# Two graph layers: row sums written over adj's transpose, a norm placed later, a copy moved to ScalarE

## The chip, the cores and the metric

One core of a Trainium2 chip runs the kernel. The metric is the device time in microseconds, the median of several executions. Beside it stands one profiled execution, from which all durations are taken.

TensorE is PE in the profile (PEld is its weight load), VectorE DVE, ScalarE ACT, GpSimd POOL, SyncE SP. L12 means line 12 of the kernel before.

## The reference

64 graphs of 256 nodes with 256 features go through two layers, each with a residual and a layer norm. Cut to what matters:

```python
# layer 0
deg = adjacency_matrix.sum(axis=-1)
deg = jnp.where(deg != 0, deg, 1.0)
d_inv_sqrt = deg ** (-0.5)
norm_adj = d_inv_sqrt[:, :, None] * adjacency_matrix * d_inv_sqrt[:, None, :]
a_plus = norm_adj + alpha_eff * jnp.eye(N)
h = jnp.einsum('bnm,bmf->bnf', a_plus, x)
x = _layernorm(x + jnp.einsum('bnf,pf->bnp', h, W) + b)
# layer 1
h = relu(bn1(conv1d(xc, conv1_w, 0)))            # xc: x with channels ahead of nodes
h = bn2(conv1d(h, conv2_w, 8))                   # 17 taps over the nodes
x_conv = relu(h + xc)
s = x @ w_se.T + b_se                            # 3 columns
dist = sq[:, :, None] + sq[:, None, :] - 2.0 * jnp.einsum('bnd,bmd->bnm', s, s)
A = jnp.exp(-dist) * adj
x_nmp = jnp.einsum('bnm,bmd->bnd', A, relu(x @ w_msg.T + b_msg))
x = _layernorm(x + gru(concat([x_conv, x_nmp]), x))
```

## The kernel before

Everything is float32. The 64 graphs run in four groups of 16 (Q = 16). A graph's work is written as Python generators, whose `yield`s are the places where other work is put in between.

- `layer0(g)` loads are two graphs deep (`loads`, two buffers for adj_t and x_t). Row sums of adj (`degrees`, L357: two ACT instructions with `accum_out`, whose written output isn't used), deg and adeg on DVE (L368, L372), deg to the power -0.5 on POOL (L370). TensorE transposes adj (L379), ACT copies it to adjT (L380; blocks 0 and 2 of each row of three), DVE puts the diagonal in the middle block (L382), ACT scales x (L392). Then p_hT (L400), hT (ACT, L405), p_out (L410), the residual on DVE (L415). `layernorm` takes statistics on DVE (L326 to L328), the root on POOL (L329), a product on DVE (L332), and applies them on ACT (L334); x1 goes to memory (L421).
- `layer1(g)` transposes x1 (L430) to xn (L434 on DVE, L435 on ACT), then p_conv (L450) with two readers on ACT (h L453, scols L454), p_msg (L471, msg L474 on ACT), a Fourier transform of tiles of h (p_dft, L486, copied out by ACT in L491), p_rows (L499: transposes of the three columns and their squares). Rows 0 to 63 of p_rows go to dist_l by ACT (L501), rows 64 to 127 to dist_r: by ACT (L504) for the 12 graphs in `ALONE` (16 to 27), by DVE (L506) for the other 52. p_dist (L513) multiplies them, ACT takes the exponential (L514), DVE multiplies with adjT (aT, L515), p_nmp (L522) and its copy (L526) end the layer.
- The 17-tap convolution is a product in the frequency domain (`products`, p_k L548) once for each group, with transforms on DVE (L598 to L735). `gru(g)` follows (p_g, L874, with sums on POOL, L845).
- In the first group, `weights` computes the transform of the convolution's weights as "other" work between the pieces: taps scaled on DVE (L300), p_u (L308), copied to u_set by ACT (L311), a difference on DVE (L313), a sum on POOL (L314), written out by POOL's queue (L316).

adjT has three buffers, x1 two, the banks for p_rows, p_dist and others four in common (`ps`).

`graphs` sets the order: while layer1 of graph i runs, layer0 of graph i + 2 is taken forward one piece at the places that `PLACES` names. Its last part, the applied norm, is kept in `ENDS` and run during the next graph's layer1, before that one's piece number `APPLIED` is followed by others. The order in which instructions stand on each engine is then settled by a scheduler when the kernel is built: it takes whatever is ready by its own reckoning, in order of its place in the program, so that an instruction may stand earlier or later than the text has it. L357 of a graph stands one or two graphs ahead of its transposes in this way, since its output `unused` is always free.

Of the kernel before, what the change touches and what calls it, by code (L numbers as in the profile page):

```python
# [10 lines left out]
AF = mybir.ActivationFunctionType  # L11
# [3 lines left out]
P = 128  # L15
# [11 lines left out]
def kernel(  # L27
# [27 lines left out]
    nc = tc.nc  # L55
# [291 lines left out]
    def layer0(g):  # L347

        a_t, x_t = ain.pop(g), xin.pop(g)

        adjT = work.tile([P, NCH, 3, P], F32, name="adjT", bufs=3)
        ADJT[g] = adjT

        deg = small.tile([P, NCH], F32, name="deg")
        def degrees():
            for c in range(NCH):
                nc.scalar.activation(  # L357
                    unused, a_t[:, c, :], AF.Copy,
                    accum_out=deg[:, c : c + 1],
                )  # L360

        if g == 1:

            with tc.issue_after(X_SCALED[0]):
                degrees()
        else:
            degrees()
        nc.vector.scalar_tensor_tensor(deg, deg, 0.0, deg, op0=ALU.is_equal, op1=ALU.add)  # L368
        dis = small.tile([P, NCH], F32, name="dis")
        nc.gpsimd.tensor_tensor(dis, deg, neg_half[:, :NCH], op=ALU.pow)  # L370
        adeg = small.tile([P, NCH], F32, name="adeg")
        nc.vector.tensor_scalar(adeg, deg, alpha_t, None, op0=ALU.mult)  # L372

        p = bank("p_adjT").rearrange("p (c n) -> p c n", c=NCH)
        for mc in range(NCH):
            for c in range(NCH):
                nc.tensor.transpose(p[:, mc, c * P : (c + 1) * P], a_t[:, c, mc * P : (mc + 1) * P], ident)  # L379
        copied = nc.scalar.copy(adjT[:, :, 0:3:2, :], p.rearrange("p c (n q) -> p c n q", q=P))  # L380
        for mc in range(NCH):
            DIAGONAL[g] = nc.vector.scalar_tensor_tensor(  # L382
                adjT[:, mc, 1, :], ident, adeg[:, mc : mc + 1], adjT[:, mc, 2 * mc, :],
                op0=ALU.mult, op1=ALU.add,
            ).ins


        x1 = work.tile([P, NCH, D], F32, name="x1")
        X1[g] = x1
        with tc.issue_after(copied.ins) if g < 2 else ExitStack():  # L390
            for c in range(NCH):
                X_SCALED[g] = nc.scalar.activation(x1[:, c, :], x_t[:, c, :], AF.Copy, scale=dis[:, c : c + 1]).ins  # L392
        nc.gpsimd.tensor_tensor(x_t, x_t, b0_t.unsqueeze(1).to_broadcast([P, NCH, D]), op=ALU.add)  # L393

        yield
        hT = work.tile([P, DCH, N], F32, name="hT", bufs=1)
        p = bank("p_hT").rearrange("p (k n) -> p k n", k=DCH)
        for k in range(DCH):
            for mc in range(NCH):
                nc.tensor.matmul(  # L400
                    p[:, k, :], x1[:, mc, k * P : (k + 1) * P],
                    adjT[:, mc, 1 - mc : 3 - mc, :].rearrange("p n q -> p (n q)"),
                    start=mc == 0, stop=mc == NCH - 1,
                )
        nc.scalar.copy(hT, p)  # L405
        yield
        p = bank("p_out0").rearrange("p (c o) -> p c o", c=NCH)
        for c in range(NCH):
            for k in range(DCH):
                nc.tensor.matmul(  # L410
                    p[:, c, :], hT[:, k, c * P : (c + 1) * P], w0[:, k, :], start=k == 0, stop=k == DCH - 1
                )
        for c in range(NCH):
            mark(
                nc.vector.scalar_tensor_tensor(  # L415
                    x1[:, c, :], p[:, c, :], dis[:, c : c + 1], x_t[:, c, :], op0=ALU.mult, op1=ALU.add
                )
            )
        yield
        yield from layernorm(x1)  # L420
        nc.scalar.dma_start(x1_d[g // Q][g % Q].rearrange("(c p) d -> p c d", p=P), x1)  # L421
        yield
# [14 lines left out]
    def layer1(g, place):  # L437

        if g not in XN:
            x1_transposed(g)  # L440
        xn, adjT = XN.pop(g), ADJT.pop(g)
        x1T = xn[:, 0 : 2 * DCH : 2 * DCH - 1]
        yield

        h = work.tile([P, NCH, D], F32, name="h", bufs=1)
        cols = scols.rearrange("p c (q r) -> p c q r", r=32)
        for c in range(NCH):
            p = bank("p_conv1")[:, : D + NSE]
            for k in range(DCH):
                nc.tensor.matmul(  # L450
                    p, x1T[:, k, c * P : (c + 1) * P], wc1[:, k, :], start=k == 0, stop=k == DCH - 1
                )
            nc.scalar.activation(h[:, c, :], p[:, :D], AF.Relu)  # L453
            nc.scalar.copy(cols[:, c, :, :NSE], p[:, D:].unsqueeze(1).to_broadcast([P, 4, NSE]))  # L454

        s3 = cols[:, :, 0, :NSE]
        sq3 = small.tile([P, NCH, NSE], F32, name="sq3")
        nc.vector.scalar_tensor_tensor(sq3, s3, -1.0, s3, op0=ALU.mult, op1=ALU.mult)
        nsq = small.tile([P, NCH], F32, name="nsq")
        nc.vector.tensor_reduce(nsq, sq3, AX.X, ALU.add)  # L460
        last = nc.vector.tensor_scalar(
            cols[:, :, 2:4, NSE], nsq.unsqueeze(2).to_broadcast([P, NCH, 2]), 0.5, None, op0=ALU.mult
        )
        mark(last)
        mark(last)
        yield
        msg = work.tile([P, NCH, D], F32, name="msg", bufs=1)
        p = bank("p_msg").rearrange("p (c d) -> p c d", c=NCH)
        for c in range(NCH):
            for k in range(DCH):  # L470
                nc.tensor.matmul(  # L471
                    p[:, c, :], x1T[:, k, c * P : (c + 1) * P], wmsg[:, k, :], start=k == 0, stop=k == DCH - 1
                )
        mark(nc.scalar.activation(msg, p, AF.Relu))  # L474
        yield


        mid = GT // 2
        if TILES[0] is not V:
            AWAY.append(place)  # L480
        for k in range(DCH):
            p = bank("p_dft")

            for c, t0, t1 in ((0, 0, mid + 1), (1, mid - 1, GT)):
                first = t0 + 1 - c * mid
                nc.tensor.matmul(  # L486
                    p[:, t0 * FL : t1 * FL], h[:, c, k * P : (k + 1) * P],
                    fwd[:, first : first + t1 - t0, :].rearrange("p t f -> p (t f)"),
                    start=c == 0, stop=True, skip_group_check=c == 1,
                )  # L490
            nc.scalar.copy(  # L491
                TILES[0][:, :, k, place * GT : (place + 1) * GT],
                p[:, : GT * FL].rearrange("p (t f) -> p f t", f=FL),
            )

        yield
        p = bank("p_rows")
        for c in range(NCH):
            nc.tensor.transpose(p[:, c * P : (c + 1) * P], scols[:, c, :], ident)  # L499
        dl = work.tile([64, N], F32, name="dist_l", bufs=1)  # L500
        nc.scalar.copy(dl, p[0:64, :N])  # L501
        dr = work.tile([64, N], F32, name="dist_r", bufs=1)
        if g in ALONE:
            nc.scalar.copy(dr, p[64:P, :N])  # L504
        else:
            nc.vector.tensor_copy(dr, p[64:P, :N])  # L506
        yield

        aT = work.tile([P, NCH, 2, P], F32, name="aT", bufs=1)
        for c in range(NCH):  # L510
            rows = slice(32 * c, 32 * c + 32)
            p = bank("p_dist")[:, :N]
            nc.tensor.matmul(p, dl[rows, c * P : (c + 1) * P], dr[rows, :], start=True, stop=True)  # L513
            nc.scalar.activation(aT[:, c].rearrange("p n q -> p (n q)"), p, AF.Exp, bias=nsq[:, c : c + 1], scale=2.0)  # L514
        mark(nc.vector.tensor_mul(aT, aT, adjT[:, :, 0:3:2, :]))  # L515
        yield
        if g in ALONE:
            x1_transposed(g + 1, True)
        p = bank("p_nmp").rearrange("p (k n) -> p k n", k=DCH)
        for k in range(DCH):  # L520
            for mc in range(NCH):
                nc.tensor.matmul(  # L522
                    p[:, k, :], msg[:, mc, k * P : (k + 1) * P], aT[:, mc].rearrange("p n q -> p (n q)"),
                    start=mc == 0, stop=mc == NCH - 1,
                )
        nc.scalar.copy(xn[:, 1 : 1 + DCH], p)  # L526
        nc.scalar.dma_start(xn_d[g], xn)
        yield
# [460 lines left out]


    PLACES = (("other",), ("layer0",), (), (), ("layer0",), ("other", "layer0"), ())
    STATS, APPLIED = len(PLACES) - 1, 2
    ENDS = [iter(())]

    def graphs(first, part, others):
# [219 lines left out]
```

## Time and profile before

| | us |
|---|---|
| median of 3 executions | 2115.55 |
| lowest and highest | 2112.75, 2115.77 |
| the profiled execution | 2121.38 |
| its span, first to last instruction | 2119.6 |

The span by stage, from PE's work: the first group's graphs with the weights until about 300 us, its frequency products with graphs 16 to 27 in between until about 520, then graphs and GRU steps in turn, and from about 1660 us only GRU steps and the last group's products. The two costliest groups of instructions, with count, total and mean time, and the idle time of the engine ahead of them:

```profile
L874 PE MATMUL p_g<-wall,sums 128*128 128x384 f32 x1536 | 538.8, 491 | 7.2 <-DVE G L901 7.2
L874 PE MATMUL p_g<-wall,inputs 128*128 128x384 f32 x1152 | 407.4, 490 | 14.3 <-DVE G L892 14.3
```

And what ACT waited for at the row sums, in total, how many times, and the longest:

```profile
ACT unused L357 <- DMA adj_t<-in_adj_dram: 41.0, 24, 5.2
```

The mean granted clock of TensorE was 0.986 of full speed.

### The profile page before, as it was taken

What the parts mean: (1) busy time and instruction counts of PE and PEld (TensorE: products, weight loads), DVE (VectorE), ACT (ScalarE), POOL (GpSimd) and SP (SyncE); (2) the same over time, 40 slices, a digit from 0 to 9 for tenths busy, and PEclk for the clock granted to TensorE, in tenths of its full rate; (3) what the DMA queues carried; (4) which work ended last, traced back from release to release, by engine and by line L of the source; (5) the groups of instructions that cost most, each with busy time, mean ns of one, the idle gap of its engine ahead of it and who ended that gap; (6) DMA issues with size and microseconds to landing.
All of it is one profiled execution on the core that took longest, in us unless ns stands there. A gap on an engine that the chain in (4) does not pass through costs nothing. (4 is left out here: it accounts for less than half of the span.)

```text
span 2119.6 us, 26193 instructions
## 1 busy us (share of the span) xinstructions
PE 2012.2 (95%) x8157; PEld 1448.3 (68%) x8157; DVE 1463.9 (69%) x3333; ACT 906.1 (43%) x2128; POOL 671.3 (32%) x672
## 2 busy tenths in 40 slices
PE   6999899999999999999999999999999999999997
PEld 5888678877667756767667765667767765555554
DVE  5555368676468788873546888885444889976776
ACT  4666543477431233555453123455444123333333
POOL 3445310121431243323221233332322124334453
PEclk9999899999999999999999999999999999999999
DMA  4765556545437644344325654434332855443331
GB/s 122 221 221 186 156 164 224 173 135 157 129 106 220 200 128 119 124 121 119 95 90 157 202 173 125 134 108 126 100 90 80 250 152 149 115 116 94 95 95 55
DMA packets 305289, 298.05 MB, mean 141 GB/s; under 512 B 84192, under 2 KB 283956, under 8 KB 305150
## 3 DMA queue, kind: packets, MB, share of 16 engines
q1 hardware_dynamic: 245198, 200.37, 32.3%
q10 hardware_dynamic: 44480, 67.39, 8.9%
q0 software_dynamic: 15472, 28.61, 6.1%
q8 instruction: 66, 1.08, 0.2%
q14 instruction: 73, 0.60, 0.1%
HBM read 193.19 MB, written 103.06 MB: 140 GB/s over the span
## 5 line engine op out<-in xcount | busy, mean ns | idle before, releaser
L874 PE MATMUL p_g<-wall,sums 128*128 128x384 f32 x1536 | 538.8, 491 | 7.2 <-DVE G L901 7.2
L874 PE MATMUL p_g<-wall,inputs 128*128 128x384 f32 x1152 | 407.4, 490 | 14.3 <-DVE G L892 14.3
L874 PEld LDWEIGHTS p_g<-wall,sums 128*128 128x128 f32 x1536 | 285.2, 191 | 197.5 <-issue 16.7
L874 PEld LDWEIGHTS p_g<-wall,inputs 128*128 128x128 f32 x1152 | 217.2, 191 | 166.8 <-DVE G L892 23.8
L845 POOL TENSOR_TENSOR sums<-inputs 128x384 f32<-128x384 f32 x128 | 139.5, 1090 | 342.4 <-PE p_g L874 314.0
L329 POOL TENSOR_TENSOR ln_rs<-ln_rs,neg_half 128x2 f32<-128x2 f32 x129 | 95.0, 737 | 391.4 <-DVE ln_rs L328 303.5
L916 ACT ACTIVATE G<-G 128x512 f32<-128x512 f32 x128 | 80.9, 632 | 263.1 <-DVE G L903 144.1
L548 PE MATMUL p_k<-u,VM 128*128 128x256 f32 x736 | 175.8, 381 | 2.4 <-DMA u<-ud 2.4
L548 PEld LDWEIGHTS p_k<-u,VM 128*128 128x128 f32 x736 | 139.4, 191 | 29.4 <-issue 2.7
L400 PE MATMUL p_hT<-adjT,x 128*128 128x256 f32 x512 | 129.9, 397 | 11.1 <-ACT msg L474 6.2
L370 POOL TENSOR_TENSOR dis<-deg,neg_half 128x2 f32<-128x2 f32 x64 | 47.3, 738 | 290.4 <-DVE deg L368 290.0
L450 PE MATMUL p_conv<-wc,xn 128*128 128x259 f32 x512 | 128.2, 391 | 11.5 <-DVE xn L434 10.6
L393 POOL TENSOR_TENSOR x_t<-x_t,b_t 128x512 f32<-128x512 f32 x64 | 94.4, 1476 | 135.8 <-issue 111.4
L410 PE MATMUL p_out<-w,hT 128*128 128x256 f32 x512 | 126.3, 390 | 1.8 <-ACT hT L405 1.3
L486 PE MATMUL p_dft<-fwd,h 128*128 128x240 f32 x512 | 117.0, 372 | 11.2 <-ACT scols L454 11.2
L522 PE MATMUL p_nmp<-aT,msg 128*128 128x256 f32 x512 | 122.6, 382 | 0.5 <-DVE aT L515 0.5
L450 PEld LDWEIGHTS p_conv<-wc,xn 128*128 128x128 f32 x512 | 96.3, 192 | 38.2 <-DVE xn L434 15.5
L471 PE MATMUL p_msg<-wmsg,xn 128*128 128x256 f32 x512 | 121.6, 380 | 0.0
L334 ACT ACTIVATE x_g<-x_g,ln_mr,ln_rs 128x256 f32<-128x256 f32 x128 | 71.0, 597 | 112.0 <-DVE ln_mr L332 110.2
L410 PEld LDWEIGHTS p_out<-w,hT 128*128 128x128 f32 x512 | 97.8, 194 | 29.4 <-ACT hT L405 9.5
L845 POOL TENSOR_TENSOR sums<-inputs,sums 128x384 f32<-128x384 f32 x64 | 69.1, 1079 | 146.6 <-PE p_g L874 146.3
L400 PEld LDWEIGHTS p_hT<-adjT,x 128*128 128x128 f32 x512 | 96.0, 198 | 27.9 <-ACT msg L474 10.9
(163 smaller groups left out, 3545.5 us busy)
## 6 DMA issues: line engine op xcount, KB each, us to landing
u<-ud SPq DMA_DIRECT2D x284, 256.0 KB
xn_d<-xn ACTq DMA_DIRECT2D x64, 512.0 KB
inputs<-xn_d SPq DMA_DIRECT2D x64, 512.0 KB
ud<-u_set POOLq DMA_DIRECT2D x39, 480.0 KB, 6.7
adj_t<-in_adj_dram SPq DMA_DIRECT2D x64, 256.0 KB
x_t<-in_x_dram SPq DMA_DIRECT2D x64, 256.0 KB
x_d<-x ACTq DMA_DIRECT2D x64, 256.0 KB
xc_d<-VM SPq DMA_DIRECT2D x64, 256.0 KB
```

What stands on the lines that cost most here:

```text
L329: nc.gpsimd.tensor_tensor(rs[:, : len(chunks)], rs[:, : len(chunks)], neg_half[:, : len(chunks)], op=ALU.pow)
L393: nc.gpsimd.tensor_tensor(x_t, x_t, b0_t.unsqueeze(1).to_broadcast([P, NCH, D]), op=ALU.add)
L400: nc.tensor.matmul(p[:, k, :], x1[:, mc, k * P : (k + 1) * P], adjT[:, mc, 1 - mc : 3 - mc, :].rearrange("p n q -> p (n q)"), start=mc == ...
L410: nc.tensor.matmul(p[:, c, :], hT[:, k, c * P : (c + 1) * P], w0[:, k, :], start=k == 0, stop=k == DCH - 1)
L450: nc.tensor.matmul(p, x1T[:, k, c * P : (c + 1) * P], wc1[:, k, :], start=k == 0, stop=k == DCH - 1)
L471: nc.tensor.matmul(p[:, c, :], x1T[:, k, c * P : (c + 1) * P], wmsg[:, k, :], start=k == 0, stop=k == DCH - 1)
L486: nc.tensor.matmul(p[:, t0 * FL : t1 * FL], h[:, c, k * P : (k + 1) * P], fwd[:, first : first + t1 - t0, :].rearrange("p t f -> p (t f)") ...
L522: nc.tensor.matmul(p[:, k, :], msg[:, mc, k * P : (k + 1) * P], aT[:, mc].rearrange("p n q -> p (n q)"), start=mc == 0, stop=mc == NCH - 1,)
L548: nc.tensor.matmul(p[:, j * D : (j + 1) * D], v[:, k, :], u[:, k, :], start=k == 0, stop=k == DCH - 1)
L845: nc.gpsimd.tensor_tensor(S[i], x, y, op=op)
L874: nc.tensor.matmul(p[:, : 3 * HD] if k == 0 else p[:, HD:], a[:, k], wall[:, b, k].rearrange("p t d -> p (t d)"), start=first and k == 0, ...
L916: nc.scalar.activation(rz, rz, AF.Tanh, scale=0.5)
```

## The change

Three edits. For the first 16 graphs the unused output of the row sums goes to the first two blocks of adjT of the same graph, which the copy L380 and the diagonal L382 later write over. The copy to dist_r is done by ACT for all graphs. The part of layer 0 behind its statistics (L332, L334, L421) is run at piece 4 of the next graph's layer1, after the copies of p_rows, instead of at piece 2, after p_msg.

```diff
         def degrees():
             for c in range(NCH):
                 nc.scalar.activation(
-                    unused, a_t[:, c, :], AF.Copy,
+                    unused if g >= Q else adjT[:, c, 0:2, :].rearrange("p n q -> p (n q)"), a_t[:, c, :], AF.Copy,
                     accum_out=deg[:, c : c + 1],
                 )
...
         dr = work.tile([64, N], F32, name="dist_r", bufs=1)
-        if g in ALONE:
-            nc.scalar.copy(dr, p[64:P, :N])
-        else:
-            nc.vector.tensor_copy(dr, p[64:P, :N])
+        nc.scalar.copy(dr, p[64:P, :N])
         yield
...
     PLACES = (("other",), ("layer0",), (), (), ("layer0",), ("other", "layer0"), ())
-    STATS, APPLIED = len(PLACES) - 1, 2
+    STATS, APPLIED = len(PLACES) - 1, 4
```

## The prediction

> **What bounds the kernel now.** I read the page's head first, then what TensorE waits for, then the dist_r tile, then the timeline of the two longest stalls.
>
> ```profile
> span 2119.6 us, 26193 instructions
> PE 2012.2 (95%) x8157; PEld 1448.3 (68%) x8157; DVE 1463.9 (69%) x3333; ACT 906.1 (43%) x2128; POOL 671.3 (32%) x672
> ```
>
> TensorE is busy for 95% of the span. A change pays only where TensorE stands still, or where its clock falls. All idle time of PE is about 107 us (2119.6 - 2012.2). The waits of TensorE (total, times, longest):
>
> ```profile
> PE p_g L874 <- DVE G L892: 14.3, 14, 3.0
> PE p_dist L513 <- DVE dist_r L506: 11.3, 10, 2.8
> PE p_dft L486 <- ACT scols L454: 11.2, 7, 2.3
> PE p_conv L450 <- DVE xn L434: 10.6, 9, 2.4
> ...
> PE p_hT L400 <- ACT msg L474: 6.2, 7, 4.5
> ```
>
> The change can touch the second line (dist_r), and whatever a late row sum (L357) delays. From the tile view of dist_r:
>
> ```profile
> L506 DVE COPY dist_r<-p_rows x52: 425/426/427, 41.6 to 1638.5; 64x256 f32<-64x256 f32 x52
> L504 ACT COPY dist_r<-p_rows x12: 369/370/371, 315.5 to 510.6; 64x256 f32<-64x256 f32 x12
> ...
>   ACT dist_l L501: 98.2, 40
> ```
>
> The last line says that DVE waited 98.2 us in front of dist_r for ACT's dist_l: the two copies read one bank and already run one after the other. The 11.3 us are thus no measure of the gain. Most of it is dist_l itself being late. The longest case, in the timeline:
>
> ```profile
> 237.66 0.42 ACT L357 ACTIVATE unused<-adj_t 128x256 f32<-128x256 f32 x1 [3.41 <-DMA adj_t<-in_adj_dram]
> 238.08 0.46 ACT L491 COPY VM<-p_dft 128x384 f32<-128x384 f32 x1
> 238.44 0.37 ACT L501 COPY dist_l<-p_rows 64x256 f32<-64x256 f32 x1
> 238.84 0.42 DVE L506 COPY dist_r<-p_rows 64x256 f32<-64x256 f32 x1 [5.34 <-ACT dist_l L501]
> 239.31 0.70 PE L513 MATMUL p_dist<-dist_r,dist_l 32*128 32x256 f32 x4 [2.83 <-DVE dist_r L506]
> ```
>
> ACT waits 3.41 us for the landing of an adj_t that is needed only two graphs later, and dist_l stands behind it. The windows view (us, then busy time per engine, clock, DMA) shows the sequel, a half clock:
>
> ```profile
> 235.35:240.70 5.35, 2.52 (x14) 1.62 (x13) 0.83 (x3) 2.67 (x9) 0.71 (x1) 1.00 0.29 96
> 240.70:244.10 3.40, 3.40 (x10) 2.63 (x9) 1.12 (x2) 1.36 (x3) 0.39 (x1) 0.50 0.03 6
> ```
>
> An ordinary graph of the first group, D = start of its p_dist = 125.78:
>
> ```profile
> 126.51 0.84 ACT L514 ACTIVATE aT<-p_dist,nsq 128x256 f32<-128x256 f32 x2
> 127.24 0.41 ACT L357 ACTIVATE unused<-adj_t 128x256 f32<-128x256 f32 x1
> 127.38 0.69 DVE L515 TENSOR_TENSOR aT<-aT,adjT 128x512 f32<-128x512 f32 x1 [1.11 <-ACT aT L514]
> ...
> 128.19 1.05 ACT L311 COPY u_set<-p_u 120x512 f32<-120x512 f32 x2
> ...
> 129.28 1.23 DVE L313 TENSOR_TENSOR u_set<-u_set,u_set 120x1024 f32<-120x1024 f32 x1 [0.50 <-ACT u_set L311]
> 129.32 3.40 POOL L314 TENSOR_TENSOR u_set<-u_set,u_set 120x1024 f32<-120x1024 f32 x1
> ```
>
> From L313 a DVE chain (L415, L326, L327, L328, L434) ends in xn at 133.19, 3.91 us after L313 starts. p_conv needs xn and could start at 133.64: 0.45 us of room.
>
> **What the Trainium skill says.** "TensorE: Matmul & The Clock Gate", on HAM oscillation, says that a TensorE gap over about 3.4 us lets the clock fall to half. The trace agrees in kind: 3.4 us at 0.50 after the stall at 239.31, and 10.2 us after the one at 258.69. It isn't strict: shorter stalls also did it (1.95 us at 420.02), and others of 2.45 us did not. "SBUF — State Buffer", in Who interferes with whom, says that a VectorE instruction with two SBUF inputs and a GpSimd instruction that reads SBUF lock each other out, the first holding the port. The trace agrees: L300 takes 1.21 us normally, and 3.37 us when it starts at 65.14 under POOL's L314 (64.04 to 67.43). "Perfetto Trace Analysis", Identifying the Most-Contended Engine, warns that matmul busy share isn't distance to the limit. So I price a stall as the time between two starts less the usual spacing (0.216 us for 256 columns: eight in 1.89 us, the last 0.38 long) and not busy time.
>
> **Part 1, row sums over adjT (g < 16).** The operations and their 0.42 us stay. Their output now needs a slot of adjT. There are three, and the oldest is freed by the aT product L515. In the built order of instructions the row sums of each graph therefore move back by about one graph: behind the exps and the first u_set copy, before the second. No queue of SP or POOL changes its sequence, save the small L370.
> Gains. At graph 12 the row sums of graph 15 and 16 stand behind the first u_set copies instead of ahead of dist_l: the stall at 239.31 (2.99 us against the usual spacing, 0.09 normal) goes, -2.9, and the 3.4 us at half clock after it, -1.7. The stall before p_conv at 228.74 (0.97, u_set copies behind a row sum that waited 1.46 for DMA) goes, -0.95. Two graphs in between with such waits of 0.6 us and 0.23 us longer spacing (15.88 against 15.65): -0.35 in all. At the start graph 1's second row sum comes before its adjT copy, so its x is ready earlier: -0.4 of 0.86.
> Costs. Row sums start at D+2.34 (after L515), the second u_set copy ends at D+3.88, and L313 starts at D+3.93 instead of D+3.50. The 0.45 us of room just covers that: nothing in graphs 2 to 11. At graph 0 the row sums used to stand before p_dist; now L313 slips 0.8 and p_conv at 49.87 waits 0.8 more. At graph 1 the taps product L300 moves ahead of L313, so L313 falls under POOL's L314 and ends about 1.2 later than the chain does now: +1.2, and the stall of 1.5 at 68.56 (p_u for taps) only moves to p_conv.
> The 4.69 us stall at 258.69 (ACT msg behind graph 17's row sum, which waits 5.23 for DMA) stays: graphs from 16 on keep their place, and the load is still issued about 9 us before.
> Sum: -2.9 -1.7 -0.95 -0.35 -0.4 +0.8 +1.2 = -4.3 us.
>
> **Part 2, dist_r by ACT (52 copies).** The wait between the two copies falls from 33 to 12 ns (the 12 copies of L504 show it) and the copy from 426 to 370 ns: 77 ns where dist_r ends the wait of p_dist and DVE was idle. Over nine such graphs 0.69, and 0.11 from two where the stall is smaller. Where DVE was busy with other work first, more goes: 0.91 at 612.25 (dist_r 0.87 us behind dist_l), 0.52 and 0.53 at 830.17 and 1343.01 (1.3 us behind, the whole stall), 0.28, 0.27, 0.12, 0.12 and 0.05 at 294.63, 1130.93, 875.21, 1388.05 and 1639.00. Sum -3.6. On ACT 52 x 0.37 = 19 us are added. They lie in the wait for p_hT (hT starts at its end in most graphs) or for L823's inputs; where hT has no room (0.05 us in graphs 41, 57 and 59) it could cost 0.37 each: taken at +0.5, bounds 0 and +1.1. At 957 and 1471 the built order puts L515 ahead of a late row sum on DVE: -0.6 for two stalls of p_nmp.
>
> **Part 3, norm at piece 4.** The scheduler moves only four norms (graph indexes near 418, 524, 792 and 1305 us). At 420.02 dist_l and dist_r come 0.6 earlier, but hT now stands behind norm and row sum and p_out comes 0.45 later: +0.45. At 526 exps come 0.4 earlier: -0.25. The other two move 33 us back, into 1.14 us of ACT idle time before 828.03: nothing, at most 0.5 each way. Sum +0.2.
>
> Total -4.3 -3.6 +0.5 -0.6 +0.2 = -7.8 us. Against the profiled execution, 2121.38 -> 2113.6. That execution lay 5.8 us above the median of 2115.55, so I carry the difference: 2107.7.
>
> **Rivals.** (a) Given back: half-clock stretches fall elsewhere once all phases shift. The trace has 47.8 us of them between 60 and 2100 us, 3.4 us each in nine places, each worth 1.7; two or three more, or the u_set room overdrawn by 0.4 us in ten graphs, leave 2113. For it: stalls of the same length are hit or not. Against: two long stalls fewer. (b) More: graph 17's load lands early enough once graph 15 and 16 are off ACT, and 4.7 us of stall with 5.1 of half clock go too: 2098. For it: other adj_t loads land within 3.2 us (307.04 to 310.2). Against: its place relative to POOL's writes of ud is unchanged. (c) Slower: POOL's L314 wins the port over L313. Today L313 starts 40 ns earlier. If the row sums, which now wait for L515, push adeg (L372, ahead of L313 on DVE) behind the start of L314, L313 waits out 3.4 us instead of taking 1.2, 2.2 more in each of ten graphs: +22 on the forecast, 2130. It decides from the point where L313 is later than D+4.3, when POOL's L370 ends; I have D+3.93. (d) The change not acting as it says: part 3 does little in the built order, already priced.
>
> **How the numbers follow.** Forecast 2107.7, own range 2102 to 2112, chance 0.64 (0.58 of it beyond 0.2%); (a) 0.14 (0.12 of it within); (b) 0.10; (c) 0.12. 0.2% is 4.2 us, about what repeated measurements can tell from no change. Faster 0.58+0.10+0.02 = 0.70, same 0.06+0.12 = 0.18, slower 0.12. The range 2096 to 2118 takes in (a) and (b) and leaves out (c).
>
> **What would show it.** Right: no wait of L513 near 236, ACT's L357 waiting for adj_t less than 41.0 us in all, p_dist's wait for dist_r at 5 us or less, L313 near D+3.9 in 1.23 us. Wrong: L313 at 3.4 us in many graphs, p_conv's wait for xn above 15 us, p_out waiting for hT by several us, or the 258.69 stall gone.

## The result and the profile after

| | before | after |
|---|---|---|
| median of 5 executions each, us | 2115.77 | 2103.45 |
| lowest and highest, us | 2112.75, 2117.18 | 2101.34, 2108.64 |
| profiled execution, us | 2121.38 | 2108.64 |
| its span, us | 2119.6 | 2106.8 |
| mean granted clock in it | 0.986 | 0.989 |

The ratio is 0.995 with a 95% interval of 0.993 to 0.997. The forecast was 2107.7, in a range of 2096 to 2118. Lines behind L503 stand three lower in the kernel after (dist_r is L503, p_dist L510, aT L512, p_g L871). One of the 14 executions of e3 below fell in a slower state of the chip (2325.9 us at a clock of 0.848) and is left out throughout.

The head of the page after:

```profile
span 2106.8 us, 26312 instructions
PE 2004.8 (95%) x8157; PEld 1444.7 (69%) x8157; DVE 1437.3 (68%) x3281; ACT 923.4 (44%) x2180; POOL 668.0 (32%) x672
```

DVE lost 26.6 us and ACT gained 17.3, mostly the 52 copies. Neither says where 12.8 us of span went. The waits (total, times, longest) say more:

```profile
ACT unused L357 <- DMA adj_t<-in_adj_dram: 32.3, 19, 3.8
...
PE p_conv L450 <- DVE xn L434: 13.1, 12, 2.4
...
PE p_dist L510 <- ACT dist_r L503: 6.7, 7, 3.1
...
PE p_hT L400 <- ACT msg L474: 3.1, 7, 1.5
...
PE p_out L410 <- ACT hT L405: 2.1, 5, 0.7
```

The row sums' wait for loads fell from 41.0 to 32.3 us, p_dist's wait for dist_r from 13.6 (11.3 and 2.3) to 6.7, p_hT's wait for msg from 6.2 to 3.1 and from 4.5 to 1.5 at the longest. p_conv waits 2.5 us more.

By place: stalls, as time between two starts of TensorE less the usual spacing (half clock included), sum to 151.6 us before and 138.8 after. Between 60 and 300 us they fall from 26.3 to 14.1, so this one stretch, where the first group's graphs run beside the weights, holds 12.2 of the 12.8 us between these two executions. From 300 us on the sums are 109.9 and 109.5. How much of the 12.2 us belongs to the change, and how much to the one execution before, only the profiles of the experiments can tell.

Graph 12 after the change, in the timeline. It is the place of the stall at 239.31 in the prediction. Here and in the timelines below, work between the lines shown is left out:

```profile
233.48 0.37 ACT L503 COPY dist_r<-p_rows 64x256 f32<-64x256 f32 x1
234.56 0.70 PE L510 MATMUL p_dist<-dist_r,dist_l 32*128 32x256 f32 x4
...
236.89 0.42 ACT L357 ACTIVATE adjT<-adj_t 128x256 f32<-128x256 f32 x1
...
238.17 0.42 ACT L357 ACTIVATE unused<-adj_t 128x256 f32<-128x256 f32 x1
238.30 1.23 DVE L313 TENSOR_TENSOR u_set<-u_set,u_set 120x1024 f32<-120x1024 f32 x1
...
238.76 2.98 POOL L314 TENSOR_TENSOR u_set<-u_set,u_set 120x1024 f32<-120x1024 f32 x1
```

Both row sums (graphs 15 and 16) now stand behind p_dist, and by then their loads have landed: no idle time stands in brackets behind L357. dist_r ends 0.7 us ahead of p_dist. L313 starts at D + 3.74 (D is again the start of the graph's p_dist) in 1.23 us, as it does in all of graphs 5 to 12.

### The profile page after: what moved, and what is told of

It is laid out like the page before. It is cut to its first block, busy times and chain, and to the rows that moved or that the text cites. A ratio compares the mean times of both kernels' runs of the same rounds, so it can differ in the third digit from the quotient of the medians.

```text
span 2106.8 us, 26312 instructions
## 1 busy us (share of the span) xinstructions
PE 2004.8 (95%) x8157; PEld 1444.7 (69%) x8157; DVE 1437.3 (68%) x3281; ACT 923.4 (44%) x2180; POOL 668.0 (32%) x672
## 5 line engine op out<-in xcount | busy, mean ns | idle before, releaser
L871 PE MATMUL p_g<-wall,sums 128*128 128x384 f32 x1536 | 541.4, 493 | 8.0 <-DVE G L898 8.0
L871 PEld LDWEIGHTS p_g<-wall,sums 128*128 128x128 f32 x1536 | 286.3, 192 | 199.4 <-issue 17.6
L871 PE MATMUL p_g<-wall,inputs 128*128 128x384 f32 x1152 | 406.3, 489 | 14.5 <-DVE G L889 13.8
L871 PEld LDWEIGHTS p_g<-wall,inputs 128*128 128x128 f32 x1152 | 216.9, 190 | 167.0 <-DVE G L889 22.9
L512 DVE TENSOR_TENSOR aT<-aT,adjT 128x512 f32<-128x512 f32 x64 | 45.6, 712 | 124.4 <-ACT aT L511 124.3
L334 ACT ACTIVATE x_g<-x_g,ln_mr,ln_rs 128x256 f32<-128x256 f32 x128 | 70.8, 596 | 111.0 <-DVE ln_mr L332 106.7
L410 PEld LDWEIGHTS p_out<-w,hT 128*128 128x128 f32 x512 | 95.9, 191 | 30.5 <-ACT hT L405 11.9
```

The source lines that it names most:

```text
L410: nc.tensor.matmul(p[:, c, :], hT[:, k, c * P : (c + 1) * P], w0[:, k, :], start=k == 0, stop=k == DCH - 1)
L871: nc.tensor.matmul(p[:, : 3 * HD] if k == 0 else p[:, HD:], a[:, k], wall[:, b, k].rearrange("p t d -> p (t d)"), start=first and k == 0, ...
```

## The experiments

Executions of one kernel spread by over 20 us on a chip (the kernel before: 2102.4 to 2126.4 in 48). Most of that is the granted clock. Over the 325 executions of the experiments that are counted here, a least-squares fit with one slope, and an offset for each kernel on each chip, gives 1.93 us less span for each 0.001 of mean clock (0.16 either way), and leaves a scatter of 2.8 us. The column "at equal clock" is what is left of a difference once this is taken out; its bounds are two standard errors. A stall may itself bring half clock on, so a part of a true gain can lie in the clock and be taken out with it. Each group of runs on one chip (e1 to e4, e5 to e8, e9 to e11, e12) has its own executions of the kernel before: 48, 52, 37 and 12.

| kernel | n | mean less before, us | clock less before | at equal clock, us |
|---|---|---|---|---|
| e1 part 1 alone | 11 | -9.3 | +0.0017 | -6.1 (1.9) |
| e2 part 2 alone | 22 | -2.1 | -0.0002 | -2.8 (1.4) |
| e3 part 3 alone | 13 | -0.3 | -0.0002 | -0.7 (1.8) |
| e4 parts 2 and 3 | 14 | -1.3 | -0.0002 | -1.8 (1.7) |
| e5 place alone | 22 | -8.1 | +0.0012 | -5.7 (1.4) |
| e6 to graph 17 | 17 | -9.1 | 0.0000 | -9.1 (1.6) |
| e7 all graphs | 14 | +0.3 | -0.0011 | -1.9 (1.7) |
| e8 chosen graphs | 12 | -9.8 | +0.0003 | -9.3 (1.8) |
| e9 the change again | 16 | -10.7 | +0.0020 | -6.8 (1.7) |
| e10 behind u_set | 22 | +6.8 | -0.0007 | +5.4 (1.5) |
| e11 graphs 47 and 51 too | 6 | -15.8 | +0.0018 | -12.4 (2.5) |
| e12 e11 without part 3 | 7 | -13.8 | +0.0010 | -11.9 (2.7) |

### The parts one by one

**e1**, only

```diff
-                    unused, a_t[:, c, :], AF.Copy,
+                    unused if g >= Q else adjT[:, c, 0:2, :].rearrange("p n q -> p (n q)"), a_t[:, c, :], AF.Copy,
```

> Part 1 alone: row sums of graphs 0 to 15 written over adjT; dist_r and the norm as before. Theory A (part 1 carries the change, and it also shortens the stall near 258.69, which the prediction had left in place): 9 to 13 us below the kernel before, all of it ahead of 300 us in the trace; the stalls at 239.31 and 258.69 shrink from 2.99 and 4.69 us to under 0.3 and under 2 us. Theory B (the parts weigh as the prediction had them): about 4 us below, the stall near 258 still over 4 us. Theory C (the gain is the fall of half-clock stretches, which any shift of phase deals anew): anywhere between -8 and +3 us, and the parts don't add up to the whole.

**e2**, only

```diff
-        if g in ALONE:
-            nc.scalar.copy(dr, p[64:P, :N])
-        else:
-            nc.vector.tensor_copy(dr, p[64:P, :N])
+        nc.scalar.copy(dr, p[64:P, :N])
```

> Part 2 alone: all 64 copies to dist_r by ScalarE; row sums and norm as before. Theory A: 0 to 3 us below the kernel before, the stall near 239 hardly shorter (about 2.9 us), the one near 258 still over 4 us. Theory B: 3.5 to 4.5 us below, with the small stalls of p_dist near 612, 830 and 1343 us gone. Theory C: anywhere between -8 and +5 us.

**e3**, only

```diff
-    STATS, APPLIED = len(PLACES) - 1, 2
+    STATS, APPLIED = len(PLACES) - 1, 4
```

> Part 3 alone: the norm of layer 0 applied at piece 4 in place of 2. Theories A and B: within 1 us of the kernel before, since four norms alone move in the order of instructions. Theory C: up to 5 us either way by another fall of the half-clock stretches, though almost nothing moved.

**e4**, the last two edits together

> The change without part 1: dist_r by ScalarE and the norm at piece 4, row sums to the unused tile as before. Theory A: 0 to 3 us below the kernel before, so about 10 us above the changed kernel; both long stalls near 239 and 258 us in place. Theory B: 3 to 4.5 us below. Theory C: not the sum of the runs of part 2 and part 3 alone, off by more than 3 us.

Ratios to the kernel before: e1 0.9959 (0.994 to 0.998), e2 0.9985 (0.997 to 1.000), e3 1.0005 (0.9988 to 1.0022), e4 0.9993 (0.9976 to 1.0011). Part 1 carries the change: -9.3 us of the -10.7 measured on e9's chip. Its -6.1 and e4's -1.8 at equal clock add up to -7.9, against -6.8 (1.7) for the whole, so the parts don't hide one another. This speaks against theory C; for theory B part 1 is too large. What remains for C is the clock: only kernels with the row sums moved run clearly higher (e1, e5, e9, e11, e12), but not all of these do (e6 and e8 hardly, e7 and e10 run lower), so no rule can be read from it. For e9 itself 8 to 12 us less in the median and a clock higher by 0.0015 were expected; 10.25 us and 0.0020 came.

The stalls of the first group in the profile of each kernel, us:

| | before | e2 | e3 | e4 | e1 | after | e9 |
|---|---|---|---|---|---|---|---|
| p_dist of graph 12, near 239 | 2.99 | 2.46 | 2.39 | 2.66 | none | none | none |
| p_conv of graph 13, near 242 to 248 | 0.80 | 0.80 | 0.90 | 0.80 | 1.69 | 1.68 | 1.68 |
| p_hT for msg, near 250 to 259 | 4.69 | 3.19 | 2.53 | 3.95 | 1.51 | 1.66 | 1.61 |
| graph 17's load, issue to row sum | 7.90 | 6.40 | 5.74 | 7.16 | 4.68 | 4.83 | 4.78 |
| p_u of graph 1 for taps, near 68 | 1.50 | 1.50 | 1.50 | 1.50 | none | none | none |

e2 and e4 were expected to keep more than 4 us near 258, and had 3.19 and 3.95. The profile before thus caught an execution that was bad in this stretch. By the same sum of stalls as above, 60 to 300 us holds about 18.8, 18.4 and 21.8 us in e2, e3 and e4, whose row sums stand as before, and 12.0, 14.1 and 12.4 in e1, after and e9. So some 7 of the 12.2 us between the two profiles come with the change, and the rest was that execution's. Nor do single profiles rank the kernels: that of e2 has a span of 2100.1 us, less than that of after. Half clock follows the same line in this stretch (13.7 us before, 3.4 to 6.8 in e2 to e4, none or 3.4 in e1, after and e9), but not from 300 us on, where e1, after and e9 have no less of it than e2 to e4.

The first row is as the prediction had it, and so is the mechanism: e4's ACT still waits for graph 16's load ahead of dist_l, though dist_r is ACT's own there. Its timeline:

```profile
236.94 0.42 ACT L357 ACTIVATE unused<-adj_t 128x256 f32<-128x256 f32 x1 [3.16 <-DMA adj_t<-in_adj_dram]
...
238.09 0.37 ACT L503 COPY dist_r<-p_rows 64x256 f32<-64x256 f32 x1
...
238.51 0.70 PE L510 MATMUL p_dist<-dist_r,dist_l 32*128 32x256 f32 x4 [2.49 <-ACT dist_r L503]
```

The third row is where the prediction failed. The row sum of graph 17 has not moved, yet its load lands sooner after its issue in each kernel with part 1 (4.7 to 4.8 us, against 5.7 to 7.9; 5.1 in e5 below). The issues of the transfers, before:

```profile
246.38 0.39 SPq L110 DMA_DIRECT2D x_t<-in_x_dram  x1
247.41 1.11 POOL L316 DMA_DIRECT2D ud<-u_set  x2 [0.30 <-POOL u_set L314]
247.72 0.34 ACTq L527 DMA_DIRECT2D xn_d<-xn  x1
249.75 0.39 SPq L108 DMA_DIRECT2D adj_t<-in_adj_dram  x1
...
257.65 0.42 ACT L357 ACTIVATE unused<-adj_t 128x256 f32<-128x256 f32 x1 [5.23 <-DMA adj_t<-in_adj_dram]
```

and after:

```profile
240.38 0.39 SPq L110 DMA_DIRECT2D x_t<-in_x_dram  x1
241.29 0.34 ACTq L524 DMA_DIRECT2D xn_d<-xn  x1
242.03 1.11 POOL L316 DMA_DIRECT2D ud<-u_set  x2 [0.30 <-POOL u_set L314]
244.24 0.39 SPq L108 DMA_DIRECT2D adj_t<-in_adj_dram  x1
...
249.07 0.42 ACT L357 ACTIVATE unused<-adj_t 128x256 f32<-128x256 f32 x1 [2.21 <-DMA adj_t<-in_adj_dram]
```

The adj_t load stands 2.03 us behind the 512 KB of xn_d before, and 2.95 after, with xn_d now ahead of the 960 KB of ud. The 0.9 us come from the second row of the table: p_conv of graph 13 stalls 0.8 to 0.9 longer, and the load waits for graph 15's transposes, which stand behind it. That gives part of the gain; the rest is that the same bytes move faster there, 8.7 us from the x_t issue to the row sum against 11.3. e3 also has xn_d ahead of ud, with 2.13 us, and lands in 5.7. Counted from the first of these two writes, the row sum comes after 7.6 to 7.9 us in the four kernels with xn_d first (e1, e3, after, e9), and after 9.7 to 10.2 in the three with ud first (before, e2, e4). No run changes the order alone. That the order of the writes makes the rate is thus suggested, not shown.

### The place or the buffer

**e5**: the output stays `unused`; the row sums of graphs 3 to 15 are put by hand behind an ACT instruction, the exponentials of the graph three earlier.

```diff
-            degrees()
+            with tc.issue_after(AT[g - 3]) if 3 <= g < Q else ExitStack(): degrees()
...
-            nc.scalar.activation(aT[:, c].rearrange("p n q -> p (n q)"), p, AF.Exp, bias=nsq[:, c : c + 1], scale=2.0)
+            AT[g] = nc.scalar.activation(aT[:, c].rearrange("p n q -> p (n q)"), p, AF.Exp, bias=nsq[:, c : c + 1], scale=2.0).ins
```

> The kernel before, with the row sums still written to the unused tile, but for graphs 3 to 15 issued behind the exponentials of the graph three earlier, which is about where part 1 puts them. Theory A (the place of the row sums in ScalarE's queue is what counts): 6 to 9 us below the kernel before, the stall of p_dist near 239 gone and that of p_hT near 250 under 2 us; the taps product stands behind L313 again, so its stall of 1.5 us near 68 is back. Rival (the other output, adjT in place of one shared tile, is what helps): within 2 us of the kernel before.

Graph 12 in its timeline, with the row sum still written to `unused`:

```profile
234.81 0.70 PE L513 MATMUL p_dist<-dist_r,dist_l 32*128 32x256 f32 x4
235.54 0.84 ACT L514 ACTIVATE aT<-p_dist,nsq 128x256 f32<-128x256 f32 x2
236.27 0.41 ACT L357 ACTIVATE unused<-adj_t 128x256 f32<-128x256 f32 x1
```

Ratio 0.9967 (0.9953 to 0.998); -5.7 at equal clock, like e1's -6.1. The stall near 239 is gone, the one near 251 is 1.97, and that at 68.52 is back with 1.73. So the place in ACT's queue is what helps; adjT is only the means that gives it.

**e10**: the output is `unused` as in e5, with parts 2 and 3. Graphs 3 to 15 stand behind a later place, the second u_set copy; graphs 16 and 17 behind the exponentials of the graph three earlier.

```diff
-                nc.scalar.copy(us[i][:, j : j + 2], p[:m])
+                UC.append(nc.scalar.copy(us[i][:, j : j + 2], p[:m]).ins)
...
-            degrees()
+            with tc.issue_after(UC[-3] if g < 15 else UC[-1] if g == 15 else AT[g - 3]) if 3 <= g < Q + 2 else ExitStack(): degrees()
```

> The change with the row sums written to the unused tile again but, for graphs 3 to 17, issued behind the second u_set copy in place of ahead of it. Theory A (the row sums ahead of the second copy make L313, the chain to xn and p_conv of graph 13 late): the stall of p_conv near 242 falls from 1.68 us to about 0.8, that at 50 from 1.36 to 0.9, none for msg near 250; 1 to 3 us below the run with the row sums of 16 and 17 over adjT (e6). Rival (those 0.9 us are covered next by another wait on the way to p_conv): the same as e6 within 1 us.

A clear miss: ratio 1.003 (1.0012 to 1.0047), slower than the kernel before. L313 starts earlier, at D + 3.27, but ten stalls of p_conv of 1.09 us stand between 90 and 241 us, and 2.8 at 52 and 258. One of the ten, in the timeline:

```profile
134.37 1.23 DVE L313 TENSOR_TENSOR u_set<-u_set,u_set 120x1024 f32<-120x1024 f32 x1 [0.98 <-ACT u_set L311]
134.41 3.39 POOL L314 TENSOR_TENSOR u_set<-u_set,u_set 120x1024 f32<-120x1024 f32 x1 [6.75 <-ACT u_set L311]
135.51 2.31 DVE L368 SCALAR_TENSOR_TENSOR deg<-deg 128x2 f32<-128x2 f32 x1
137.74 0.86 DVE L415 SCALAR_TENSOR_TENSOR x<-p_out,dis,x_t 128x256 f32<-128x256 f32 x2
```

L368, an instruction on two columns of 0.16 us, takes 2.31: it ends with POOL's L314, and L415 and the whole chain to xn wait behind it on DVE. In the changed kernel L368 stands ahead of L313, where it costs nothing. This is rival (c) of the prediction with another victim. The Trainium skill has the mechanism in "SBUF — State Buffer", Who interferes with whom: a VectorE instruction with two SBUF inputs contends with a GpSimd one that reads SBUF. The trace agrees, and the price here is what is left of the GpSimd instruction (2.29 us when L368 starts), however small the other is.

### Further row sums

**e6** and **e7** change the condition: `g >= Q + 2`, and no condition at all. **e8** adds graphs 17, 24, 34, 41, 47, 51, 57 to the first 16. **e11** has `unused if (g >= Q + 2 and g not in (47, 51)) else adjT...`, and **e12** is e11 with APPLIED at 2.

> The whole change, with the condition at graph 18 in place of 16, so that graphs 16 and 17 write over adjT too. Theory A (msg of graph 13 still stands behind graph 17's row sum, which waits for its load): the stall of 1.66 us near 250 goes and no p_hT waits for msg there; 1 to 3 us below the changed kernel. Rival (the wait only moves on): the same time as the changed kernel within 1 us, with p_conv near 257 or 272 later by as much.

> The whole change, with every graph's row sums over adjT. Theory A (a row sum ahead of its load costs the same at later graphs): the stalls near 568 (3.31 us), 1037, 1119 (1.15 and 1.23), 404, 927 and 1439 (0.6 to 0.74) go with that near 250: 5 to 10 us below the changed kernel. Rival (behind the aT product the row sums come too late where no weights work lies between, and transposes, diagonals and p_hT wait): 0 to 10 us above the changed kernel, with p_hT waiting for DVE's adjT over 5 us in all.

> The whole change, with graphs 17, 24, 34, 41, 47, 51 and 57 writing over adjT besides the first 16: those whose row sum waits for its load ahead of a stall of TensorE. Theory A: the same seven stalls go, 9.3 us in all by the profile of the changed kernel, less a third that comes back elsewhere: 4 to 9 us below the changed kernel. Rival: the stall moves to the next wait in line at each place: within 2 us of the changed kernel.

> The change with row sums over adjT for graphs 16, 17, 47 and 51 too. Theory A (at 47 and 51 nothing else was late, as the run with the chosen graphs showed): the stalls of 1.1 to 1.2 us near 1037 and 1119 go, less 0.8 us that comes back at p_hT near 1340: 1 to 2 us below e6. Rival: the same as e6 within 1 us.

> The kernel of e11 without part 3: the norm at piece 2 as before, row sums over adjT for graphs 0 to 17, 47 and 51, dist_r by ScalarE. Theory A (part 3 does nothing in company either, and the gain of the further row sums stands without it): 12 to 17 us below the kernel before, 9 to 12 us at equal clock. Rival (the applied norm in front of the copies of p_rows is late work that part 3 takes away once the row sums are gone): 3 us or more slower than e11, so 8 to 12 us below the kernel before, with p_dist waiting for dist_l or dist_r longer by as much.

e6 (0.9958, 0.9945 to 0.9971): the stall of 1.66 us near 250 is gone, nothing took its place, and at equal clock it is 2.3 us (2.3) below e9, on another chip. Its mean clock is that of the kernel before, so its mean time is no better than the change's. The stall of p_conv near 242 is 1.36 in place of 1.68, since graph 16's L368 and L372 no longer stand in the chain to xn there.

e7 (1.0008, 0.9992 to 1.0025) gives the gain back (at equal clock -1.9 is left), as its rival had it: row sums wait for the aT product, ACT's later work and DVE's diagonals slip behind, and p_hT waits for adjT (L382) 11.9 us in place of 4.7, with seven such stalls of 0.8 to 1.5 us between 402 and 488:

```profile
PE p_hT L400 <- DVE adjT L382: 11.9, 14, 1.6
```

e8 (0.9952, 0.9936 to 0.9967) is 2.5 us (2.5) below e9 at equal clock, not the 4 to 9 expected. Of seven stalls those near 250, 1037 and 1119 are gone. At graph 34 the stall of 3.31 us near 568 became one of 2.87. After:

```profile
566.49 0.42 ACT L357 ACTIVATE unused<-adj_t 128x256 f32<-128x256 f32 x1 [3.76 <-DMA adj_t<-in_adj_dram]
...
568.06 1.22 PE L510 MATMUL p_dist<-dist_r,dist_l 32*128 32x256 f32 x4 [3.15 <-ACT dist_r L503]
```

and in e8:

```profile
563.65 0.70 PE L510 MATMUL p_dist<-dist_r,dist_l 32*128 32x256 f32 x4
567.62 0.91 ACT L820 ACTIVATE inputs<-inputs,bn_bias 128x256 f32<-128x256 f32 x2 [4.69 <-POOL inputs L817]
568.55 0.59 ACT L405 COPY hT<-p_hT 128x512 f32<-128x512 f32 x1
...
569.19 1.99 PE L410 MATMUL p_out<-w,hT 128*128 128x256 f32 x8 [2.71 <-ACT hT L405]
```

p_dist goes through, and ACT then stands at L820, which waits 4.69 us for POOL, where it waited 3.76 us for the row sum's load before. hT behind it is late, and with it p_out. The wait moved to the next in line. Near 404 and 927 nothing changed, near 1439 the stall grew from 0.60 to 1.84, and two of 1.35 came up at 429 and 443, where p_hT waits for adjT.

e11 (0.9923, 0.9892 to 0.9953) and e12 (0.9933, 0.9907 to 0.9958) keep only 16, 17, 47 and 51. Both are ahead of the change: -12.4 and -11.9 at equal clock against -6.8. e11 ran on e9's chip, and is 5.6 us (2.7) below it at equal clock, though with 6 executions its interval of the ratio still touches e9's (0.9953, 0.9933 to 0.9972). It is 3.3 us (2.9) below e6, where 1 to 2 were expected. In its profile the stalls near 1037 and 1119 are gone and p_hT near 1339 waits 0.80 longer, as expected; that is worth under 2 us, so the trace does not account for all of the 3.3. e12 differs from e11 by 0.5 us (3.6), on another chip: part 3 shows no effect in company either, but one of 3 us could hide in that.

## Why the prediction was right, and where it was wrong

The direction and the mechanism of its main step held; the size came out short, -7.8 against -10.7 (e9) and -12.3 (the five executions). Taken apart, the short term is the clock: without its -1.7 the forecast is -6.1, against -6.8 (1.7) at equal clock, while the clock's own part is 3.9 in e9. That the rest comes so near is in part luck, since misses in both directions cancel. By its steps:

**Stall at 239.31, -2.9: right.** None in e1, after and e9.

**Half clock after it, -1.7: right for this profile (e2 and e4 have it too, e3 not), with a cost beside it unpriced.** From the start of p_dist of graph 12 to that of p_conv took 8.84 us before and 7.25 in e3, where the row sums are unchanged but this stretch stayed at full clock: 1.6 us. It took 8.03 in e1 and after, again at full clock, so part 1 adds 0.78 here. L313 starts at D + 3.74 against e3's D + 3.27, and graph 16's L368 and L372 now stand within the chain to xn (3.70 us from L313 to L434 against 3.39). The prediction had the cover for this, the p_u of the next weights, in graphs 2 to 11; at graph 12 the weights end and nothing covers it. In the mean over executions the clock's part is larger than 1.7: 3.2 us in e1 (0.0017), 3.9 in e9 (0.0020). After the stall near 258, the profile before had 10.2 us at half clock, e3 and e4 3.4, e2 and the changed kernel none. Rival (a) expected half clock to come back elsewhere; e1, e5 and e9 speak against it, e6, with no higher mean clock, does not. Its 47.8 us at half clock between 60 and 2100 us are 44.4 by the trace (eight stretches of 3.4, one of 6.8, one of 10.2).

**p_conv at 228.74, -0.95, and the spacing of two graphs, -0.35: gone, but not shown to be the change's.** Neither is seen after; p_dist of graphs 5 to 12 starts about every 15.65 us. But the stall at 228.74 is absent in e2, e3 and e4 too, with the row sums unmoved; e2 and e4 have one of 0.48 and 0.62 elsewhere, e3 none. It was mostly this execution's.

**Graph 1's x, -0.4: wrong, and small.** The stall at 32.82 went from 1.00 to 0.91.

**Graph 0, +0.8: right in kind, too large.** p_conv waits 1.36 in place of 0.90, +0.46.

**Graph 1, +1.2, stall at 68.56 "only moves": wrong, by 2.5 us.** Before, L300 stood behind L313 and L314:

```profile
63.99 1.22 DVE L313 TENSOR_TENSOR u_set<-u_set,u_set 120x1024 f32<-120x1024 f32 x1 [0.97 <-ACT u_set L311]
64.04 3.39 POOL L314 TENSOR_TENSOR u_set<-u_set,u_set 120x1024 f32<-120x1024 f32 x1 [4.80 <-ACT u_set L311]
65.14 3.37 DVE L300 TENSOR_TENSOR taps<-taps,scale 85x1024 f32<-85x1024 f32 x1
```

After:

```profile
64.74 1.22 DVE L300 TENSOR_TENSOR taps<-taps,scale 85x1024 f32<-85x1024 f32 x1 [0.41 <-issue]
64.81 4.50 POOL L314 TENSOR_TENSOR u_set<-u_set,u_set 120x1024 f32<-120x1024 f32 x1
65.88 1.22 DVE L313 TENSOR_TENSOR u_set<-u_set,u_set 120x1024 f32<-120x1024 f32 x1
...
66.95 1.89 PE L308 MATMUL p_u<-taps,dft_w 85*120 85x256 f32 x8
```

The order is as foretold, but L313 is not held up: it takes 1.22 us although L314 has been under way for 1.07. L314 is the one that waits. It takes 4.50 us and ends 2.21 after L313's end. So p_u has its taps, the 1.50 goes, and p_conv near 69 stalls 0.43 in place of 0.25.

**Graphs 2 to 11, nothing: right but for one.** In graphs 3 and 5 to 11 L313 starts at D + 3.74 where 3.93 was worked out, 1.23 us each. In the profile after, graph 7's row sum met its load 1.46 us late between the u_set copies of graph 4, and p_conv stalled 1.14 at 117; e1 and e9 don't have it.

**Stall at 258.69, "stays": wrong, the other large miss.** It fell to 1.66. The reason was half given in rival (b), which happened in part: the load lands sooner, probably since what stands ahead of it moved. The step also took one profiled execution's 4.69 as the kernel's own; e2 to e4, with the row sums unchanged, had 2.5 to 4.0. So 1 to 2.5 us of real gain, and 3.0 in the two profiles compared.

**Part 2, -3.6 + 0.5 - 0.6: right within its measurement**, -2.8 (1.4). The single places agree: p_dist's stall at graph 31 (612 before) falls from 1.28 to 0.35, at graphs 32 and 48 (830, 1343) from 0.63 to 0.10. The cost on ACT exists, but not at hT of graphs 41, 57 and 59: p_dist of graphs 37 and 53 stalls about 0.4 longer in the profile after, in waits that end with a VM copy of ACT (L491). The p_nmp stalls near 960 and 1474 went from 0.2 to none.

**Part 3, +0.2: not to be told from nothing**, e3 -0.7 (1.8). Its one visible trace is at graph 20, where p_dist no longer stalls (1.95 at 420.02 before, 1.01 in e1) but p_out does, by 0.79 near 407 (0.80 in e3); p_hT's stall there is 0.74, and was 0.69.

With the two misses and the unpriced cost put in, the sum is -7.8 - 2.5 - 2.0 (taking 2.0 for 258.69) + 0.8 = -11.5, near what was measured. The nearness proves little: without the clock's 1.7 it is -9.8, against 6.8 (1.7) at equal clock. Some of the difference is what was priced from one bad execution, as at 228.74.

Of the signs, all of the right ones came but one: p_dist waits 6.7 us for dist_r, not 5 or less, 3.1 of them at 568. Of the wrong ones one came, the shrunk stall at 258.69. The carried difference between profiled execution and median was sound: its clock of 0.986 lay below the 0.989 or so that the kernel before has on average.

## What to carry to other kernels

A cheap instruction whose output is always free may be put far ahead in an in-order queue, and then waits there for a load with everything behind it. Giving it an output that comes free at the right moment moves it back; how far back matters to half a microsecond, and the same edit on all graphs gave nothing. Before a single stall of a profile is priced, ask how much of it is this execution's, and ask of a half-clock stretch what it hides.

## What was not expected of the hardware

- Who gets the port between two VectorE instructions. With L314 waiting since 45 ns after the start of L313, L314 went ahead of the following L300, which took 3.37 us in place of 1.21 (before, 65.14). With L314 waiting since 70 ns after the start of L300, L313 went ahead of L314 (after, 65.88). In all three forms seen L314 ends 2.2 us after L313's end, having started 0.05 or 0.46 us after or 1.07 us before it. Why the two differ stays open, and that L314 stood waiting, not working, is read from these times alone.
- The Trainium skill, in "TensorE: Matmul & The Clock Gate" on HAM oscillation, speaks of gaps above some 3.4 us. Here 3.4 us at half clock followed a stall of 2.46 and one of 2.66 us near 239 (e2, e4), while 2.39 at the same place left the clock at full (e3). Stalls of 2.2 to 2.3 us near 272 to 280 did it in e3 and after, and not in e1. So the length of a stall alone doesn't decide.
